# Two chained cross-attentions: VectorE's product of the semantic result moved ahead of the maxima, the sums copied right behind it, fewer unread products in the tail

## The chip, the cores and the metric

The kernel runs on one core of one Trainium2 chip. Its time is the device time of the core in microseconds (us); the number compared is the median of several runs. A profile is one execution taken by the hardware profiler: it has a start and an end for each instruction of TensorE (PE, with its weight loads PEld), VectorE (DVE), ScalarE (ACT) and GpSimd (POOL), and for the DMAs that SyncE (SP) issues.

## The reference

Two attention layers follow each other. Each has 64 batches of 256 tokens with 320 channels, and 20 heads of 16. All is float32. Layer 0 attends to 77 text tokens. (Its image part has no tokens: the context has 77 rows, all of them text.) Layer 1 takes the last 4 of the 77 as image tokens and the other 73 as text:

```python
# layer 0
q, k, v = heads(x @ Wq.T), heads(ctx @ Wk.T), heads(ctx @ Wv.T)
x = x + merge(softmax(q k^T / 4) v) @ Wo.T + bo
# layer 1
text, ip = ctx[:, :-4], ctx[:, -4:]
probs_t  = softmax(q k_t^T / 4)                 # 73 text tokens
text_out = probs_t v_t
qsem     = l2norm(probs_t @ text)               # per head, 512 wide
sem      = qsem @ l2norm(ip)^T                  # 4 numbers per head and token
probs_ip = softmax(q k_ip^T / 4 + 0.5 * sem) * spatial_mask
x = x + (text_out + probs_ip v_ip) @ W_out + b_out
```

## The kernel before, in words

The 64 batches go in 32 pairs p. A pair is cut into 10 units for each layer: a unit is 8 heads (or, for the last heads, 4 heads of both halves) of 128 tokens of one batch. The main loop runs over steps g; k = g % 10 is the place in the period. In step g layer 0 works on unit g and layer 1 on unit g - 13 (`LAG` is 13). The code calls layer 0 and layer 1 `l` = 0 and 1.

The semantic part of layer 1 doesn't compute `qsem` in 512 channels. A Gram matrix of the context (`gram`, `place_gram`: line L512 and the copies L516, L517) stands in tile `gv` beside the values and a column of ones. The matmuls of `semantics` (L774, L781) multiply the transposed exponentials of the step before with it and give, per head, 73 columns (exponentials times Gram matrix, the *semantic result*) and 21 more columns (products with the image rows, the values and the sum). `weighted` multiplies the 73 columns on VectorE with the exponentials (`prod`, L792 and L795), a later reduction (`nrm`, L1130) makes the squared norm of it, and `sums_out` copies the other 21 columns on ScalarE (`sums`, L1057).

One PSUM tile, `sc`, of 4 banks, takes all of a step: the semantic result of the unit that is one step further, and the scores of both layers (L659). There is a single buffer of it, so the matmuls of the next step wait until all readers of this step have done. The readers of `sc` are, for each layer, the maxima (`mx`, L677) and the difference from them (`w`, L679), both on VectorE and both in `shifted`; the product; and the copy of the sums.

The order of each engine's instructions is that of the program: `keep_order` ties each instruction to the one before it on its engine. Within a step it is this, in the kernel before:

- TensorE: `sc` (semantics, scores of layer 0, scores of layer 1); the transposes of layer 1's exponentials (`tr`, `rtr`: L723, L724); the first fillers; the transposes of layer 0's normalized exponentials; the second fillers, and for some units the value products `pv` (L809, L814, in `attend`).
- VectorE: `mx`, `w` of layer 0; `mx`, `w` of layer 1; at k = 1 and 6 the maxima `most` (L890) of the image scores; the product; the sums `sm` of layer 0's exponentials (L705), their reciprocal (L706); `nrm`; then, at some k, the small work of the image part, and the additions of the projections to `x` (L617, four in a row, and L636).
- ScalarE: copies left from the step before (queries L602, outputs L945 and L946); `pt` and `pr` of layer 1 (the copies of its transposes out of PSUM, L730 and L731); the exponential of layer 0 (L687); copies of the first fillers (`kT` L348, `q` L589, `vs` L391, `gram` L516 and L517); `pt` and `pr` of layer 0 (L749 and L750, or L738 and L741); the copy of the sums; the exponentials of layer 1 (`parts`, L690 and L691); copies of the second fillers and of `pv`; every fifth step a square root (L875) and back to the exponential (L877), each with a load of its function table. At k = 5 the exponential of layer 0 stands behind the layer-0 copies. At k = 1 and 6 the copy of the sums stands ahead of the layer-0 copies.
- GpSimd: placing of keys and values, `att` (L694, reads layer 1's `w`), and the products `parts` of layer 0 (L710), which wait for `sm`.

*Fillers* are the projections that lie around the attention: keys, queries, values, outputs, Gram matrices. `fillers(k, p)` lists them by k in three groups. Their PSUM tiles come from two pools with two buffers each: `pms` (projections `k_ps`, `q_ps`, `v_ps`, `o_ps`, `g_ps`, and most `pv`) and `ptr` (all transposes, `itr` L915 and `ltr` L928 among them). A matmul that takes a buffer waits for the copy that empties it: for example layer 0's transposes take the buffers of layer 1's, and wait for the copies `pt` and `pr` of these.

In the tail, when layer 0 has no unit left (from step 323 on), `keep_busy` issues transposes of the identity that nobody reads (`busy`, L759): 14 in each of 10 steps in which layer 1 still has a unit, and other numbers behind these.

Of the kernel before, what the change touches and what calls it, by code (L numbers as in the profile page):

```python
# [70 lines left out]
def tile_two_cross_attentions(ctx: ExitStack, tc: tile.TileContext, a: dict, out: bass.AP):  # L71
# [143 lines left out]
    def load_more(g):  # L215
        queue = nc.sync
        if g == 1:
            queue.dma_start(cip, cip_in.rearrange("(k p) t -> p k t", p=P))
            load_ctx_weight("wkip1", queue, wkip)
        elif g == 3:  # L220
            load_ctx_weight("wvip1", queue, wvip)
        elif g == 5:
            wo[0], bo[0] = load_out("wo0", queue), load_bias("bo0", queue)
        elif g == 6:
            wq[1] = load_chan("wq1", queue)
        elif g == 8:
            wo[1], bo[1] = load_out("wo1", queue), load_bias("bo1", queue)
            queue.dma_start(smask, a["smask"])
# [416 lines left out]
    def eight(t, u):  # L645

        return t[:, PLACES[u] : PLACES[u] + 8].rearrange("p (r e) ... -> p r e ...", e=2)
# [16 lines left out]
    def shifted(ps, l, p, b, u):  # L664


        nt = (T, TT)[l]
        name = f"{l}_{p}_{b}{u}"
        if l and u == 0:
            stats[p, b] = (  # L670
                small.tile([P, 2 * H, NIP], F32, tag="att", name=f"att{p}_{b}", bufs=3),
                big.tile([P, 2 * H, NIP + D + 1], F32, tag="sums", name=f"sums{p}_{b}", bufs=3),
                small.tile([P, 2 * H], F32, tag="nrm", name=f"nrm{p}_{b}", bufs=3),
            )
        sc = ps[:, :, 2 * T * l : 2 * T * (l + 1)].rearrange("p r (e t) -> p r e t", t=T)
        mx = small.tile([P, 4, 2], F32, tag="mx", name=f"mx{name}")
        nc.vector.tensor_reduce(mx, sc[:, :, :, :nt], AX.X, ALU.max)  # L677
        w = ws[l] = sp.tile([P, 4, 2, T], F32, tag=f"w{l}", name=f"w{name}", bufs=2 - l)
        nc.vector.tensor_tensor(  # L679
            w, sc, mx.unsqueeze(3).broadcast_to([P, 4, 2, T]), ALU.subtract  # L680
        )

    def exponential(l, g, p, b, u):

        w = ws[l]
        if not l:
            nc.scalar.activation(w, w, AF.Exp, scale=SCALE)  # L687
            return
        two = ws[l] = parts1[g % 3]
        nc.scalar.activation(two[:, :4].rearrange("p (e a) j t -> p (a j) e t", e=2), w[:, :, :, :M], AF.Exp, scale=SCALE)  # L690
        nc.scalar.activation(  # L691
            rests(two), w[:, :, :, M:TT], AF.Exp, scale=SCALE
        )
        nc.gpsimd.tensor_copy(eight(stats[p, b][0], u), w[:, :, :, TT:])  # L694

    def rests(two):

        r = two[:, 4].rearrange("p j (a c) -> p (j a) c", c=QR)
        return r[:, :, : 2 * R1].rearrange("p r (e t) -> p r e t", e=2)
# [52 lines left out]
    def keep_busy(n, pool=ptr, tag="tr"):  # L752


        if n:
            ps = pool.tile([P, 4, P], F32, tag=tag, name=f"busy{len(busy)}")
            busy.append(n)
            for i in range(n):
                nc.tensor.transpose(ps[:, i % 4, :], ident, ident)  # L759
# [26 lines left out]
    def by_block(ps):  # L786
        return ps[:, :, SEM0 : SEM0 + 2 * GV].rearrange("p r (e t) -> p r e t", t=GV)

    def weighted(ps, p, b, u, w):
        sm = by_block(ps)  # L790
        prod = sp.tile([P, 4, 2, TT], F32, tag="prod", name=f"prod{p}_{b}{u}", bufs=1)
        nc.vector.tensor_tensor(  # L792
            prod[:, :, :, :M], sm[:, :, :, :M], w[:, :4].rearrange("p (e a) j t -> p (a j) e t", e=2), ALU.mult
        )
        nc.vector.tensor_tensor(prod[:, :, :, M:], sm[:, :, :, M:TT], rests(w), ALU.mult)  # L795
        return prod
# [70 lines left out]
    def image_squares(p, b):  # L867
        total, r = stats[p, b][1][:, :, NIP + D], stats[p, b][2]
        t = small.tile([P, 2 * H], F32, tag="least", name=f"least{p}_{b}", bufs=1)
        nc.vector.tensor_mul(t, total, total)  # L870
        nc.vector.scalar_tensor_tensor(r, t, EPS * EPS, r, ALU.mult, ALU.max)

    def image_norm(p, b):
        r = stats[p, b][2]
        nc.scalar.activation(r, r, AF.Sqrt, scale=(SCALE / SEM) ** 2)  # L875

        nc.scalar.activation(one, r[:, :1], AF.Exp, scale=0.0)  # L877
# [167 lines left out]
    def unit(g):  # L1045
        return (g // NU, g % NU // BU, g % BU) if 0 <= g < NP * NU else None
# [9 lines left out]
    def sums_out(ps):  # L1056
        nc.scalar.copy(eight(stats[before1[:2]][1], before1[2]), by_block(ps)[:, :, :, TT:])  # L1057
# [3 lines left out]
    for g in range(NP * NU + LAG + 12):  # L1061
        p, k = divmod(g, NU)
        first, second, third = fillers(k, p)
        if g == NU + 3:
            in_order = len(nc.cur_bb.bb.instructions)
        load_more(g)
        now = [unit(g), unit(g - LAG)]
        ps = prod = None
        for fn, args in early.pop(g, ()):
            fn(*args)  # L1070
        drains = [fn for what in ("i", "q", "o") if what in held for fn in held.pop(what)()]
        for fn in drains:
            fn()
        if now[0] or now[1] or before1:
            ps = psc.tile([P, 4, 512], F32, tag="sc", name=f"sc{g}")
            todo = []
            if before1:
                todo.append((semantics, (*before1[:3], before1[4])))
            for l in range(2):
                if now[l]:  # L1080
                    todo.append((scores, (l, *now[l])))
            for n, (fn, args) in enumerate(todo):
                fn(ps, n == 0, n == len(todo) - 1, *args)
        ends = before1 and before1[2] == BU - 1
        for l in range(2):
            if now[l]:
                shifted(ps, l, *now[l])
        if g in middle:
            fn, args = middle.pop(g)
            fn(*args)  # L1090
        new1 = None
        if last1:
            transposed(1, *last1)
            new1 = (*last1, pts[1])
        if now[0] and k != 5:
            exponential(0, g, *now[0])
        if k == 2:
            for fn, args in first:
                fn(*args)
        if before1:  # L1100
            prod = weighted(ps, *before1[:4])
        if k != 2:
            for fn, args in first:
                fn(*args)
        if before1 and k in (1, 6):
            sums_out(ps)
        if last0:
            transposed(0, *last0)
        idle = g - NP * NU
        if idle > 2:  # L1110
            keep_busy(14 if now[1] else {13: 12, 14: 16, 15: 14, 16: 16, 17: 16}.get(idle, 0))
        if idle == 17:
            fn, args = second.pop(0)
            fn(*args)
            keep_busy(8)
        if now[0] and k == 5:
            exponential(0, g, *now[0])
        if before1 and k not in (1, 6):
            sums_out(ps)
        for fn, args in between.pop(g, ()):  # L1120
            fn(*args)
        if now[1]:
            exponential(1, g, *now[1])
        if now[0]:
            normalize(g)
        for fn, args in later.pop(g, ()):
            fn(*args)
        if before1:
            q, b, u = before1[:3]
            nc.vector.tensor_reduce(eight(stats[q, b][2], u), prod, AX.X, ALU.add)  # L1130
            if ends:
                image_squares(q, b)
                text_output(q, b)
                later[g + 1] = [(image_scores, (q, b))]
                middle[g + 2] = (image_shifted, (q, b))
                between[g + 2] = [(image_exponential, (q, b))]
                (early if b else later)[g + 3] = [(image_weights, (q, b))]
        for fn, args in second:
            fn(*args)
        if last0:  # L1140
            q, b, u, _ = last0
            if u == 1 or u == BU - 1:
                attend(q, b, int(u > 1))
        for fn, args in third:
            fn(*args)
        if g in (6, 7, 9, 10, 18, 19) or -6 <= idle <= -2:
            keep_busy(8, pms, "ms")
        if ends:
            image_norm(*before1[:2])
        last0 = (*now[0], ws[0]) if now[0] else None  # L1150
        before1 = new1
        last1 = (*now[1], ws[1]) if now[1] else None
# [51 lines left out]
```

## Time and profile before

| | us |
|---|---|
| median of 3 runs | 2474.95 (2473.02 to 2475.86) |
| the profiled execution's own time | 2474.45 |
| its span, first to last instruction | 2472.7 |
| PE busy | 2394.2 (97%) |
| DVE busy | 1987.4 (80%) |
| ACT busy | 1482.2 (60%) |
| POOL busy | 1370.9 (55%) |
| `prod` L792 and L795, mean of one | 0.681 and 0.223 |
| `mx` L677 and `w` L679, mean of one | 0.776 and 0.800 |
| `sums` L1057, mean of one | 0.301 |
| `w` L687 (exponential of layer 0), mean of one | 0.719 |
| `busy` L759, in all | 39.9 (310 transposes) |

How to read the profile. A line of the waits says who waited, for whom, then the total in us, how often, and the longest. A line of the timeline has the start in us, the duration, the engine, the line of the kernel, the operation, the tiles written and read with their shapes, and in brackets the idle time of the engine ahead of it and what ended it. Matmuls are pipelined and their ends are modelled; neighbours on one engine overlap by some hundredths of a us. The granted clock of TensorE was 0.999 of full speed.

### The profile page before, as it was taken

How to read it: one execution, taken by the hardware profiler on the slowest of the kernel's cores; microseconds unless marked ns; L12 is line 12 of the kernel's file. 1: busy time of each engine (PE TensorE's matmuls, PEld its weight loads, DVE VectorE, ACT ScalarE, POOL GpSimd, SP SyncE). 2: the span in 40 equal slices, each digit the busy share in tenths (PEclk: the TensorE clock that was granted, in tenths of full speed). 3: DMA queues.
4: the chain of work that ended last, by engine and by line, in shares of the span. 5: the costliest groups of instructions: out<-in, count | busy, mean ns of one | idle time of the engine just before them, and what ended most of it. 6: DMA issues, size and time to landing. Idle time of an engine off the chain costs nothing.

```text
span 2472.7 us, 100470 instructions
## 1 busy us (share of the span) xinstructions
PE 2394.2 (97%) x41118; PEld 1847.9 (75%) x41118; DVE 1987.4 (80%) x3673; ACT 1482.2 (60%) x3767; POOL 1370.9 (55%) x3483
## 2 busy tenths in 40 slices
PE   7899999999999999999999999999999999999888
PEld 5677777777777777777777777777777777777676
DVE  3588788888888888888888888888888888888864
ACT  3466666666666666666665666665665666666543
POOL 2455565566555656555656555556555556555542
PEclk9999999999999999999999999999999999999999
DMA  6212111112111112111121211121211121211000
GB/s 173 75 30 57 50 52 47 56 53 58 52 57 41 54 54 59 52 52 51 47 59 56 62 45 48 46 60 56 62 44 48 47 59 56 61 39 39 26 23 25
DMA packets 150914, 131.83 MB, mean 53 GB/s; under 512 B 45432, under 2 KB 129144, under 8 KB 150456
## 3 DMA queue, kind: packets, MB, share of 16 engines
q1 hardware_dynamic: 149592, 124.27, 17.5%
q8 instruction: 325, 5.32, 0.9%
q10 hardware_dynamic: 864, 1.15, 0.2%
q14 instruction: 133, 1.09, 0.1%
HBM read 87.43 MB, written 33.91 MB: 49 GB/s over the span
## 4 chain that ended last, share of the span: by engine, by line
PE 76%; DVE 12%; ACT 3%; DMA 3%; POOL 2%; issue 1%; SPq 1%; DVEq 0%; POOLq 0%; ACTq 0%
PE tr L723 10%; PE sc L774 9%; PE o_ps L547 8%; PE q_ps L547 8%; PE sc L659 7%; DVE w L679 5%; PE v_ps L390 4%; PE sc L781 4%; PE o_ps L632 3%; DVE mx L677 3%; PE k_ps L345 3%; PE pv L809 2%; PE q_ps L557 2%; PE o_ps L557 2%; PE q_ps L575 2%; PE pv L814 2%
## 5 line engine op out<-in xcount | busy, mean ns | idle before, releaser
L677 DVE TENSOR_REDUCE mx<-sc 128x8 f32<-128x584 f32 (+1 forms) x640 | 496.6, 776 | 342.1 <-PE sc L659 339.3
L710 POOL TENSOR_TENSOR parts<-w,sm 128x512 f32<-128x512 f32 (+1 forms) x640 | 440.6, 709 | 437.1 <-DVE sm L706 144.2
L679 DVE TENSOR_TENSOR w<-sc,mx 128x616 f32<-128x616 f32 x640 | 511.8, 800 | 73.0 <-DVE mx L677 1.4
L723 PE MATMUL tr<-ident,parts 128*128 128x128 f32 x2560 | 407.5, 282 | 9.5 <-ACT pt L730 5.6
L730 ACT COPY pt<-tr 128x512 f32<-128x512 f32 x320 | 187.1, 585 | 323.8 <-PE tr L723 318.9
L723 PEld LDWEIGHTS tr<-ident,parts 128*128 128x128 f32 x2560 | 284.2, 140 | 128.6 <-issue 83.1
L687 ACT ACTIVATE w<-w 128x616 f32<-128x616 f32 x320 | 230.1, 719 | 143.7 <-DVE w L679 142.7
L774 PEld LDWEIGHTS sc<-gv,pt 64*64 64x64 f32 x10240 | 233.5, 133 | 105.6 <-ACT sums L1057 52.7
L774 PE MATMUL sc<-gv,pt 64*64 64x94 f32 x10240 | 277.9, 245 | 23.6 <-ACT sums L1057 23.0
L694 POOL COPY att<-w 128x32 f32<-128x32 f32 x320 | 67.0, 209 | 354.6 <-DVE w L679 350.8
L705 DVE TENSOR_REDUCE sm<-w 128x8 f32<-128x616 f32 x320 | 250.9, 784 | 13.9 <-ACT w L687 13.8
L659 PE MATMUL sc<-kbd,q 32*64 32x154 f32 x10240 | 247.7, 293 | 1.1 <-ACT q L602 1.0
L547 PE MATMUL q_ps<-x,wq 128*128 128x256 f32 x1024 | 232.9, 380 | 5.3 <-ACT kT L348 5.3
L547 PE MATMUL o_ps<-aT,wo 128*128 128x256 f32 x1024 | 231.8, 379 | 0.7 <-ACT aT L945 0.7
L1057 ACT COPY sums<-sc 128x168 f32<-128x168 f32 x320 | 96.2, 301 | 225.8 <-DVE prod L795 223.9
L1130 DVE TENSOR_REDUCE nrm<-prod 128x8 f32<-128x584 f32 x320 | 226.7, 709 | 0.3
L792 DVE TENSOR_TENSOR prod<-sc,parts 128x512 f32<-128x512 f32 x320 | 217.9, 681 | 2.8 <-PE sc L781 2.8
L547 PEld LDWEIGHTS q_ps<-x,wq 128*128 128x128 f32 x1024 | 189.2, 190 | 30.2 <-ACT kT L348 7.3
L547 PEld LDWEIGHTS o_ps<-aT,wo 128*128 128x128 f32 x1024 | 189.6, 190 | 24.4 <-ACT aT L945 1.1
L690 ACT ACTIVATE parts<-w 128x512 f32<-128x512 f32 x320 | 206.4, 645 | 0.0
L749 ACT COPY pt<-tr 128x512 f32<-128x512 f32 x256 | 150.3, 587 | 66.9 <-PE tr L723 65.5
L390 PE MATMUL v_ps<-wv,cf 128*128 128x320 f32 (+1 forms) x624 | 179.2, 433 | 0.0
(144 smaller groups left out, 4560.3 us busy)
## 6 DMA issues: line engine op xcount, KB each, us to landing
out_dram<-x SPq DMA_DIRECT2D x64, 256.0 KB
x<-in_x_dram SPq DMA_DIRECT2D x31, 512.0 KB
v_rows<-vs SPq DMA_DIRECT2D x38, 320.0 KB
vm<-v_rows SPq DMA_DIRECT2D x152, 80.0 KB
ct<-in_ctx_dram SPq DMA_DIRECT2D x32, 308.0 KB
cf<-in_ctx_dram SPq DMA_DIRECT2D x38, 256.0 KB
g_rest<-gram_rest SPq DMA_DIRECT2D x512, 0.5 KB
v_rest<-v_rows SPq DMA_DIRECT2D x448, 11.2 KB
```

The source lines that it names most:

```text
L390: nc.tensor.matmul(ps[:n, :C], cfs[i][:, k, :n], wv[l][:, k, :], start=(k == 0), stop=(k == KE - 1))
L547: nc.tensor.matmul(ps[b][:, m, :], w[:, k, m * P : (m + 1) * P], main[:, k, b * S : (b + 1) * S], start=(k == 0 and m == 0), stop=False,)
L659: nc.tensor.matmul(ps[c, r, 2 * T * l : 2 * T * (l + 1)], tokens[rows, c], kbd[rows, part].rearrange("p e t -> p (e t)"), start=start, sto ...
L677: nc.vector.tensor_reduce(mx, sc[:, :, :, :nt], AX.X, ALU.max)
L679: nc.vector.tensor_tensor(w, sc, mx.unsqueeze(3).broadcast_to([P, 4, 2, T]), ALU.subtract)
L687: nc.scalar.activation(w, w, AF.Exp, scale=SCALE)
L705: nc.vector.tensor_reduce(sm, w, AX.X, ALU.add)
L710: nc.gpsimd.tensor_tensor(two[:, 8 * t0 : 8 * t1].rearrange("p (h t) -> p h t", h=8), w[:, :, t0:t1], sm.unsqueeze(2).broadcast_to([P, 8, ...
L723: nc.tensor.transpose(ps[:, i, :], flat[:, i * P : (i + 1) * P], ident)
L774: nc.tensor.matmul(ps[c, i % 2 * 2 + j, at : at + GV], pt[half_rows, i, c], gv[b][half_rows, part, i, :], start=start and i < 2, stop=False,)
L792: nc.vector.tensor_tensor(prod[:, :, :, :M], sm[:, :, :, :M], w[:, :4].rearrange("p (e a) j t -> p (a j) e t", e=2), ALU.mult)
L1130: nc.vector.tensor_reduce(eight(stats[q, b][2], u), prod, AX.X, ALU.add)
```

## The change

`weighted` and `sums_out` are called right behind the matmuls of `sc`, ahead of `shifted`, in every step. On VectorE the two instructions of the product come first in the step, then the maxima and differences of the layers. On ScalarE the copy of the sums stands behind the copies left from the step before and ahead of `pt` of layer 1, where it stood behind the copies of layer 0 (at k = 1 and 6: ahead of these). The special cases of k = 2 and of k = 1 and 6 go. In the tail `keep_busy` issues 8 transposes in each of the ten steps instead of 14. The numbers of all instructions but these transposes are the same.

```diff
         ends = before1 and before1[2] == BU - 1
+        if before1:
+            prod = weighted(ps, *before1[:4])
+            sums_out(ps)
         for l in range(2):
             if now[l]:
                 shifted(ps, l, *now[l])
...
         if now[0] and k != 5:
             exponential(0, g, *now[0])
-        if k == 2:
-            for fn, args in first:
-                fn(*args)
-        if before1:
-            prod = weighted(ps, *before1[:4])
-        if k != 2:
-            for fn, args in first:
-                fn(*args)
-        if before1 and k in (1, 6):
-            sums_out(ps)
+        for fn, args in first:
+            fn(*args)
         if last0:
             transposed(0, *last0)
         idle = g - NP * NU
         if idle > 2:
-            keep_busy(14 if now[1] else {13: 12, 14: 16, 15: 14, 16: 16, 17: 16}.get(idle, 0))
+            keep_busy(8 if now[1] else {13: 12, 14: 16, 15: 14, 16: 16, 17: 16}.get(idle, 0))
...
         if now[0] and k == 5:
             exponential(0, g, *now[0])
-        if before1 and k not in (1, 6):
-            sums_out(ps)
```

## The prediction

> **What bounds it now.** I read the page first, then the waits, then the timeline of whole steps. A step is one round of the main loop; ten (k = 0 to 9) make a period of 72.8 us (windows view, 1181.15 to 1253.97). R is the end of a step's last `sc` matmul; the times of steps below count from R.
>
> ```profile
> PE 2394.2 (97%) x41118; PEld 1847.9 (75%) x41118; DVE 1987.4 (80%) x3673; ACT 1482.2 (60%) x3767; POOL 1370.9 (55%) x3483
> ...
> PE 76%; DVE 12%; ACT 3%; DMA 3%; POOL 2%; issue 1%; SPq 1%; DVEq 0%; POOLq 0%; ACTq 0%
> ```
>
> TensorE is the bound, with VectorE second on the chain. So the question is who TensorE nearly waits for. The waits:
>
> ```profile
> DVE mx L677 <- PE sc L659: 339.3, 221, 14.5
> ...
> ACT sums L1057 <- DVE prod L795: 223.9, 243, 3.4
> ...
> PEld sc L774 <- ACT sums L1057: 52.7, 99, 1.6
> ...
> PEld pv L809 <- ACT pr L750: 11.5, 30, 0.4
> ...
> PEld pv L809 <- ACT gram_rest L517: 6.1, 29, 0.6
> ```
>
> The reader is to see two things. VectorE has 339.3 us of room ahead of its maxima, about 1 us a step. And TensorE is already on the edge of three ScalarE copies, with tiny waits once a period: any delay of those copies is paid in full. Now a step of k = 7 (R = 1232.50) and, last two lines, one of k = 0 (R = 1253.97):
>
> ```profile
> 1232.01 0.49 PE L659 MATMUL sc<-kbd,q 32*64 32x154 f32 x15
> ...
> 1232.58 0.80 DVE L677 TENSOR_REDUCE mx<-sc 128x8 f32<-128x616 f32 x1
> ...
> 1234.31 0.72 ACT L687 ACTIVATE w<-w 128x616 f32<-128x616 f32 x1 [0.37 <-DVE w L679]
> ...
> 1235.10 0.59 ACT L749 COPY pt<-tr 128x512 f32<-128x512 f32 x1
> ...
> 1235.74 0.88 PE L915 MATMUL itr<-ident,iw 128*80 128x128 f32 x4
> ...
> 1236.33 0.22 DVE L795 TENSOR_TENSOR prod<-sc,parts 128x72 f32<-128x72 f32 x1
> ...
> 1236.59 0.30 ACT L1057 COPY sums<-sc 128x168 f32<-128x168 f32 x1 [0.74 <-DVE prod L795]
> ...
> 1257.37 0.16 ACT L517 COPY gram_rest<-g_ps 73x13 f32<-73x13 f32 x1
> ...
> 1257.59 0.64 PE L809 MATMUL pv<-pt,v 128*32 128x256 f32 x8
> ```
>
> ScalarE works in order: the exponential L687 waits for `w` of layer 0, and behind it stand copies that free PSUM for TensorE. `itr` starts 0.05 after `pt` ends; `pv` starts 0.06 after `gram_rest`.
>
> **The change, part by part.** A plain step now: `mx` at 0.08, `w` of layer 0 ends 1.78, L687 runs 1.88-2.59, `w` of layer 1 ends 3.39, `prod` ends 4.13, `sums` 4.16-4.46, next `sc` from 4.51. The product (L792 and L795) costs 0.82 (0.08 less overlapped), whether first or last. What differs is the wait. In the built program the layer-0 maxima wait for the `sums` copy, the next `sc` for the layer-1 `w`, and the product still for the last `sc` matmul. So after: `prod` 0.08-0.90, `sums` 0.93-1.23 (the 0.03 and 0.30 of the row above), `mx` at 1.27 (0.04 on, much like the 0.05 from `sums` to the next `sc`), `w` 0 ends 2.97, L687 3.07-3.79, `w` 1 ends 4.58, next `sc` from 4.63. VectorE stands idle 0.37 a step for the copy, its later sums L705 come 0.46 later, and L687 with all behind it 1.2 later. `pt` of layer 1, now behind `sums`, ends at 1.73 instead of 1.26.
>
> That both reads take turns is how the trace has it: 243 times `sums` waited for `prod`, though `sc` had been complete for 4 us. Bounds of the handover: 0 if the readers could overlap, 0.37 as derived, 0.5 with a further 0.1; I take 0.37, from the nearest row. The Trainium skill (PSUM — Partial Sum Buffer, "PSUM bank collisions raise a hardware error") says that ScalarE and VectorE must not touch one bank and quadrant together, reads included; it speaks against this change, and without it the sum would be that of the third rival below.
>
> Step by step, with TensorE's own row first:
> k = 1 and 3: nothing. In k = 1 `o_ps` L547 keeps TensorE until 3.99; in k = 3 half of `q_ps` L547 runs until 4.43, and the copy it needs (L589) ends 4.05.
> k = 4: the layer-0 transposes began at 1.53; they need `pt`, 1.73 + 0.05: +0.25.
> k = 5: ScalarE comes from the square root's two table loads (1.28 each) and two `q` copies; these end 0.47 later, less the 0.25 by which step 4 is longer: 1.43 instead of 1.20. `sums` ends 1.66, `w` 1 ends 5.01, next `sc` 5.06 instead of 4.51: +0.55.
> k = 6: next `sc` was at 4.74, because `most` (L890) stood ahead of the product; now 4.63: -0.11. VectorE ends 0.46 later, 0.68 into step 7.
> k = 7: `prod` ends 1.50, `sums` 1.83, `w` 0 3.50, L687 4.32, `kT` 4.49, `pt` 4.97, `itr` 5.02 instead of 3.24: +1.78. In 6 of 30 periods step 6 is 8.2 long (two more `v_ps`), VectorE is in time, and it is +1.18.
> k = 8: `vs` L391 ends 4.11 (was 3.31), then `pt` 4.64; `ltr` L928 begins 4.68 instead of 4.11: +0.55; half that in the 6.
> k = 9: the next `sc` waited for `sums` (ends 5.58, behind `pt`); in k = 1, with the same matmuls, it starts 0.18 earlier: -0.18.
> k = 0: VectorE's four L617 of step 9 end at 1.70 instead of 1.06 (0.46 later, the step 0.18 shorter). From there `prod` 2.52, `sums` 2.85, `w` 0 4.59, L687 5.41, `gram_rest` 5.57, `pv` 5.62 instead of 3.63: +2.0. The largest term.
> k = 2: VectorE is 0.70 late (0.17-0.26 before; `most` and the L617 of step 1); L687 ends 4.27, `pt` 4.75, `pv` 4.80 instead of 3.79: +1.0.
>
> A full period: 2.0 + 0 + 1.0 + 0 + 0.25 + 0.55 - 0.11 + 1.78 + 0.55 - 0.18 = 5.84, or 8%. Semantic results exist from step 15, layer-0 exponentials until step 319. Count: k = 0, 29 x 2.0 = 58; k = 2, 30; k = 4, 30 x 0.25 = 7.5; k = 5, 31 x 0.55 = 17; k = 6, -2.6; k = 7, 24 x 1.78 + 6 x 1.18 + 1 = 50.8; k = 8, 14.9; k = 9, -5.4. Together +170.
>
> The rest at nothing, with its cover. GpSimd's `parts` L710 end at most 0.5-1.1 later, but the layer-0 transposes need them only 1.5 into the next step. SP issues the same DMAs in the same order; those of `gram` leave 2 us later in k = 0 and are needed by `gv` L530 eight steps on. At k = 2 `first` holds only L632 and L636, which VectorE gets after both maxima as before. The tail: 10 steps lose 6 transposes of 0.125 (1.75 for 14), 7.5 us of TensorE. But they start behind `pt`, now 0.47 later, and the next `sc` waits for `w` 1 at about 2410.85 where it had `sums` at 2410.72: nothing, within -7.5 and +3. With less fill TensorE pauses longer there; its longest wait on `pt` is now 2.2 us and the windows view still shows a granted clock of 1.00 from 2380 to 2400.
>
> The Trainium skill (TensorE: Matmul & The Clock Gate, "What's actually happening") lets the clock halve after an idle window of about 3.4 us. My pauses are 2 us at most, so by the page too nothing is added; if each period did lose one window it would be, as an estimate from that page, some 1.7 us x 30 = 51 us more.
>
> The profiled execution took 2474.45 (span 2472.7), 0.5 below the median of 2474.95. 2474.45 + 170 = 2644.5, against the median 2645.
>
> **Rivals.** First, that only VectorE's ring counts, and the copies behind L687 have more room than the edges show (a wait of 0.05 could be chance). Then only steps where VectorE is late pay: k = 0 +0.44 (`w` 1 then sets the next `sc`), k = 5 +0.13, k = 7 +0.08, k = 6 -0.11: about 0.55 x 30 = +17, 2492. Against it: the 29 and 30 waits of `pv`, once a period, and `itr`.
>
> Second, faster: the release of `sc` decides. If the maxima followed the product directly and L687's delay of 0.82 were covered, `w` 1 would end 4.13 and the next `sc` start at 4.18: k = 5 -0.33, k = 6 -0.35 (TensorE's own 4.39), k = 9 -0.18, 0.86 x 30 = 26, with 7.5 of the tail 2441. It decides once exp L687 may come 0.82 later without a wait at k = 0, 2 and 7, where the rows show 0.06, 0.44 and 0.05 of room.
>
> Third, the readers are not kept apart, but ScalarE's queue is as I read it: L687 0.8 later, k = 0 about +1.1, k = 7 +1.1, k = 2 +0.4, less the gains: about 2.1 x 30 = +65, 2540. The same time would come if the product ran beside the `sc` matmuls, the change then doing more than the built waits let it.
>
> Fourth, all handovers cost 0.1 more and the lateness piles up: seven paying steps x 0.2 x 30 = +42, 2690, or above 2705 if the layer-1 `kT` copy (0.07 of room in k = 4) also misses.
>
> **How the numbers follow.** Mine 0.77, the first rival 0.06, faster 0.04, the third 0.06, the fourth 0.06, no change 0.01. The range 2575 to 2705 takes in my sum with 40% off its terms below and the fourth rival's 2690 above. A measurement of this kernel tells about 0.2% (5 us) from no change; so faster 0.04, same 0.01, slower 0.95.
>
> **What would show it.** Right: `ACT sums <- DVE prod` falls from 223.9 us to some tens; `DVE mx <- ACT sums` appears with about 300 waits of 0.37; `DVE mx <- PE sc` goes, and `prod <- PE sc` takes its place; L687 waits longer for `w`; TensorE shows waits of 1-2 us on `gram_rest` (k = 0), `pt` at `itr` (k = 7) and at `pv` (k = 2); TensorE's share falls to about 90% at an unchanged granted clock; the period is near 78.6. Wrong: `mx` starting without the copy, `pv` and `itr` starting where they did, or a period below 75.

## The result, and the profile after

The changed kernel takes 2638.62 us (median of 4 runs, 2637.01 to 2641.29), the kernel before in the same runs 2474.39. The ratio is 1.0665, 95% interval 1.0646 to 1.0683: slower, by 164 us, where the forecast said 2645. The page, busy time and the chain that ended last:

```profile
PE 2407.9 (91%) x41058; PEld 1843.1 (70%) x41058; DVE 2011.7 (76%) x3673; ACT 1478.4 (56%) x3767; POOL 1373.5 (52%) x3483
...
DVE 45%; PE 34%; ACT 10%; issue 4%; DMA 3%; POOL 2%; SPq 1%; DVEq 0%; ACTq 0%; POOLq 0%
```

No engine does noticeably more work. TensorE's share fell from 97% to 91%, and the chain, 76% TensorE before, now runs mainly through VectorE. The waits:

```profile
ACT sums L1057 <- DVE prod L795: 486.2, 292, 4.8
ACT w L687 <- DVE w L679: 341.2, 287, 3.7
DVE prod L792 <- PE sc L659: 316.6, 201, 5.1
...
DVE mx L677 <- ACT sums L1057: 139.8, 318, 1.7
...
PE tr L723 <- ACT pt L730: 43.8, 100, 2.7
PEld pv L809 <- ACT gram_rest L517: 42.1, 29, 1.5
...
PEld pv L809 <- ACT pt L749: 33.7, 32, 1.1
PEld itr L915 <- ACT pt L749: 31.0, 30, 1.9
```

The room that VectorE had ahead of its maxima (339.3 us) now stands ahead of the product (316.6). New is the turn-taking: the maxima wait 318 times for the sums, 0.44 each. And three ScalarE copies for which TensorE's weight loads had hardly waited (6.1, 0.6 and 4.9 us in all, in the order of the lines) now hold them up by 1.0 to 1.5 us each, once a period. TensorE's transposes of layer 0 wait 100 times for `pt` of layer 1 (L730), where they waited 6 times before (5.6 us). One step of k = 7 (the last `sc` matmul ends at 1312.16), from the timeline:

```profile
1313.28 0.22 DVE L795 TENSOR_TENSOR prod<-sc,parts 128x72 f32<-128x72 f32 x1
...
1313.59 0.30 ACT L1057 COPY sums<-sc 128x168 f32<-128x168 f32 x1 [1.22 <-DVE prod L795]
...
1313.92 0.80 DVE L677 TENSOR_REDUCE mx<-sc 128x8 f32<-128x616 f32 x1 [0.42 <-ACT sums L1057]
...
1315.65 0.72 ACT L687 ACTIVATE w<-w 128x616 f32<-128x616 f32 x1 [1.10 <-DVE w L679]
...
1316.44 0.59 ACT L749 COPY pt<-tr 128x512 f32<-128x512 f32 x1
...
1317.08 0.64 PE L915 MATMUL itr<-ident,iw 128*80 128x128 f32 x4 [0.77 <-ACT pt L749]
```

This is the forecast's path link by link: product, sums, maxima, exponential, `pt`, and TensorE at the end of it. `itr` starts at 4.92 where it started at 3.24, and 5.02 was forecast. At k = 0 (that end is 1257.00) it is `gram_rest` and `pv`:

```profile
1262.34 0.16 ACT L517 COPY gram_rest<-g_ps 73x13 f32<-73x13 f32 x1
...
1262.55 0.64 PE L809 MATMUL pv<-pt,v 128*32 128x256 f32 x8 [1.20 <-ACT gram_rest L517]
```

`pv` starts at 5.55 instead of 3.63; 5.62 was forecast.

Below, a step's length is the time from the end of its last `sc` matmul to the end of the next step's, in the profiled execution, the median over the steps of one k. The steps 15 to 319 took 2248.1 before and 2412.0 after (+163.9); what lies ahead of them changed by -1.0, what lies behind by +1.6. So the loss is in the main loop.

### The profile page after: what moved, and what is told of

It is laid out like the page before. It is cut to its first block, busy times and chain, and to the rows that moved or that the text cites. A ratio compares the mean times of both kernels' runs of the same rounds, so it can differ in the third digit from the quotient of the medians.

```text
span 2637.3 us, 100892 instructions
## 1 busy us (share of the span) xinstructions
PE 2407.9 (91%) x41058; PEld 1843.1 (70%) x41058; DVE 2011.7 (76%) x3673; ACT 1478.4 (56%) x3767; POOL 1373.5 (52%) x3483
## 4 chain that ended last, share of the span: by engine, by line
DVE 45%; PE 34%; ACT 10%; issue 4%; DMA 3%; POOL 2%; SPq 1%; DVEq 0%; ACTq 0%; POOLq 0%
DVE w L679 12%; DVE mx L677 11%; DVE prod L792 6%; PE sc L774 5%; PE q_ps L547 4%; PE sc L659 4%; DVE sm L705 4%; DVE nrm L1123 3%; DVE x L617 3%; ACT sums L1057 3%; PE pv L809 3%; ACT w L687 2%; PE v_ps L390 2%; PE pv L814 2%; PE tr L723 2%
## 5 line engine op out<-in xcount | busy, mean ns | idle before, releaser
L677 DVE TENSOR_REDUCE mx<-sc 128x8 f32<-128x584 f32 (+1 forms) x640 | 497.7, 778 | 178.7 <-ACT sums L1057 139.8
L792 DVE TENSOR_TENSOR prod<-sc,parts 128x512 f32<-128x512 f32 x320 | 218.7, 684 | 322.7 <-PE sc L659 316.6
L723 PE MATMUL tr<-ident,parts 128*128 128x128 f32 x2560 | 409.9, 283 | 48.1 <-ACT pt L730 43.8
L687 ACT ACTIVATE w<-w 128x616 f32<-128x616 f32 x320 | 229.8, 718 | 341.2 <-DVE w L679 341.2
L723 PEld LDWEIGHTS tr<-ident,parts 128*128 128x128 f32 x2560 | 278.8, 141 | 185.8 <-issue 116.5
L1057 ACT COPY sums<-sc 128x168 f32<-128x168 f32 x320 | 96.0, 300 | 486.9 <-DVE prod L795 486.2
L730 ACT COPY pt<-tr 128x512 f32<-128x512 f32 x320 | 189.7, 593 | 0.7 <-PE tr L723 0.7
```

The lines of the kernel that those rows point to most:

```text
L723: nc.tensor.transpose(ps[:, i, :], flat[:, i * P : (i + 1) * P], ident)
L792: nc.vector.tensor_tensor(prod[:, :, :, :M], sm[:, :, :, :M], w[:, :4].rearrange("p (e a) j t -> p (a j) e t", e=2), ALU.mult)
```

## The experiments

### One half of the edit at a time

**The product alone.** `weighted` ahead of `shifted`, the sums where they were, 8 transposes in the tail:

```diff
+        if before1:
+            prod = weighted(ps, *before1[:4])
         for l in range(2):
             if now[l]:
                 shifted(ps, l, *now[l])
```

> The product stands ahead of the maxima in every step; the copy of the sums stays where it was, behind the layer-0 copies (k = 1 and 6: ahead of them), and so waits for the layer-1 w. The maxima follow the product without a wait. Theory 1 (ScalarE's ordered queue: the exponential L687 comes later, and TensorE pays for the copies behind it): L687 starts 0.78 later than in the kernel before, pv at k = 0 starts +0.85, itr at k = 7 +0.77, pv at k = 2 +0.2, and k = 6 gains 0.23: about +51, 2526 us. Theory 2 (VectorE's ring of maxima and product is the bound after the change, and what it lost is the wait for the copy in each step): without the wait VectorE has what it had, so 2468 to 2476 us.

Measured: 2511.16, ratio 1.0154 (1.0139 to 1.0169). **The sums alone**, with the product in its old place and 14 transposes:

```diff
+        if before1:
+            sums_out(ps)
         for l in range(2):
             if now[l]:
                 shifted(ps, l, *now[l])
```

> The kernel before, with the copy of the sums alone ahead of the maxima in every step; the product stays behind them. The maxima wait for a ScalarE copy that needs only the last matmul of sc. Theory 1: mx of layer 0 starts at 0.47 in plain steps (0.08 before), but where ScalarE comes late from the square root it waits longer, 2.25 at k = 0 and 1.55 at k = 5; steps k = 0 +1.27, 5 +1.14, 7 +0.38, 8 +0.25, 9 -0.18: +86, 2560 us. Theory 2 (the wait for the copy, each step, is what the change costs VectorE): the wait is there in full, so about the time after the change, 2620 to 2645 us.

Measured: 2546.97, ratio 1.0297 (1.028 to 1.0314). Changes of the step lengths, in us:

| k | forecast | both (the change) | product alone | sums alone |
|---|---|---|---|---|
| 0 | +2.0 | +1.92 | +0.69 | +1.17 |
| 2 | +1.0 | +1.16 | +0.15 | 0 |
| 4 | +0.25 | +0.43 | 0 | 0 |
| 5 | +0.55 | +0.31 | -0.01 | +1.29 |
| 6 | -0.11 | -0.01 | -0.22 | -0.03 |
| 7 | +1.78 | +1.44 | +0.59 | +0.34 |
| 8 | +0.55 | +0.64 | +0.13 | -0.01 |
| 9 | -0.18 | -0.23 | 0 | -0.24 |
| sum | 5.84 | 5.66 | 1.33 | 2.52 |

k = 1 and 3 are unchanged in all of them. In the main loop the product alone cost 43.6, the sums alone 76.6, both together 163.9, which is 43.7 more than the two. What the two share is room: that ahead of the copies, and VectorE's own. At k = 2 `pv` started 0.44 after `pt`: the product alone makes L687 0.80 later there and pays 0.15, the sums alone make it 0.36 later and pay nothing, and with both it is 1.81 later, more than the sum of the two, since VectorE also comes late into the step (its first reader of `sc` starts at 0.73, before at 0.17); 1.16 is paid. At k = 4 neither alone costs anything: only when the copy of the sums stands ahead of `pt` of layer 1 and itself waits for the product does `pt` come late enough for TensorE. With the product alone the same waits show, that of `pv` smaller:

```profile
PEld itr L915 <- ACT pt L749: 29.1, 30, 2.0
PEld pv L809 <- ACT gram_rest L517: 27.1, 29, 0.9
```

The sums alone hold up the maxima where ScalarE is late: at k = 0 behind a table load (`mx` starts at 2.13, though VectorE's L617 end at 1.58) and at k = 5 behind the two `q` copies (1.73 instead of 0.08). At k = 5 the product is last and ends at 5.74, and the next `sc` waits for it; the waits of `mx` in that run:

```profile
DVE mx L677 <- ACT sums L1057: 390.6, 262, 5.6
```

My expectation was 2526 and 2560; both came out about 14 lower, the other theories' 2468 to 2476 and 2620 to 2645 are far off.

### Where k = 0 loses 1.92

**The change at k = 0 alone:**

```diff
+        ahead = before1 and k == 0
+        if ahead:
+            prod = weighted(ps, *before1[:4])
+            sums_out(ps)
```

> The kernel before, with product and sums ahead of the maxima at k = 0 alone (one step in ten). Theory 1: no lateness is handed over from step 9, so pv at k = 0 starts 1.29 later instead of the 1.92 of the whole change, all other steps stay: 29 x 1.29 = 37, 2511 us. Theory 2: VectorE's ring at k = 0 ends with the layer-1 w at 5.55 where TensorE is ready at 5.51, so +0.1 a period, 2477 us.

Measured: 2511.29, ratio 1.0154 (1.0139 to 1.0169), as theory 1 had it; k = 0 is 8.48 long (+1.24), all others as before. **The changed kernel with k = 9 in its old order:**

```diff
-        if before1:
+        ahead = before1 and k != 9
+        if ahead:
             prod = weighted(ps, *before1[:4])
             sums_out(ps)
...
+        if before1 and not ahead:
+            prod = weighted(ps, *before1[:4])
...
+        if before1 and not ahead:
+            sums_out(ps)
```

> The changed kernel, but step k = 9 keeps the order of before (product behind the maxima, sums behind layer 0's copies). Theory 1 (part of what k = 0 loses is lateness of VectorE and ScalarE that step 9 hands over): k = 9 loses its gain, 7.23 to 7.46 us, and k = 0 falls from 9.16 to about 8.5, as in the version with the change at k = 0 alone (8.48); together 30 x (0.23 - 0.66) = -13 us, the time about 2626. Theory 2 (k = 0's loss is all its own): k = 0 stays at 9.16, k = 9 loses 0.23, 30 x 0.23 = 7 us, the time about 2645.

Measured: 2630.07, ratio 1.0625 (1.0609 to 1.0641). k = 9 goes from 7.23 to 7.46 and k = 0 from 9.16 to 8.45: so 0.7 of k = 0's loss is made in step 9. There VectorE ends later and TensorE earlier, and the L617 end at 1.01 instead of 1.73 into step 0. The main loop fell by 10.5; 13 was expected.

### How much is ScalarE's queue

**The exponential L687 behind the copies** that free PSUM (first fillers and `pt` of layer 0), at the six k where they are due:

```diff
-        if now[0] and k != 5:
+        if now[0] and k not in (0, 2, 4, 5, 7, 8):
             exponential(0, g, *now[0])
...
-        if now[0] and k == 5:
+        if now[0] and k in (0, 2, 4, 5, 7, 8):
             exponential(0, g, *now[0])
```

> The kernel after the change, but the exponential L687 of layer 0 stands behind the copies of the first fillers and of the layer-0 transposes at k = 0, 2, 4, 5, 7 and 8 (after the change it stands so at k = 5 alone). VectorE's order and its wait for the copy of the sums are untouched. Theory 1: TensorE's waits on gram_rest, on pt at itr and on pt at pv go, what stays is pt of layer 1 behind the sums and VectorE's lateness; steps against before k = 0 +0.75, 2 +0.5, 4 +0.4, 5 +0.3, 7 +0.75, 8 0, 9 -0.2: +75, 2550 us. Theory 2: VectorE does the same as after the change, 2630 to 2640 us.

Measured: 2577.98, ratio 1.0423 (1.0408 to 1.0439). That gives back 60.6 of the 164; theory 1 had expected 2550, and most of what is missing lies at k = 2. k = 0 falls from 9.16 to 8.21, k = 7 from 8.23 to 7.35, k = 8 from 7.87 to 7.23. TensorE's waits for these copies at `pv` and `itr` shrink to under 1 us in the whole run. But behind them the next limit stands. At k = 7, and at k = 2 too, layer 0's transposes wait for `pt` of layer 1, which stands behind the sums (at k = 7 they begin at 2.36 instead of 1.59, at k = 2 at 2.94 instead of 2.07). At k = 0 it is VectorE: `w` of layer 1 ends at 6.41, and the next `sc` starts at 6.47. At k = 2, which did not fall at all (8.33), the last wait is for L636, queued behind both maxima:

```profile
1248.24 0.48 DVE L636 SCALAR_TENSOR_TENSOR x<-o_ps,bo,x 128x256 f32<-128x256 f32 x1
...
1248.77 0.66 PE L584 MATMUL q_ps<-x,wq 128*64 128x128 f32 x8 [0.30 <-DVE x L636]
```

**L636 moved ahead of layer 1's maxima, first try.** `project_last` is called between the two layers at k = 2:

```diff
         for l in range(2):
+            if l and k == 2:
+                for fn, args in first:
+                    fn(*args)
             if now[l]:
                 shifted(ps, l, *now[l])
```

> The version with the exponential behind the PSUM-freeing copies (2577.98 us), and at k = 2 also project_last's fillers moved between layer 0's and layer 1's maxima, so that VectorE's L636 runs ahead of layer 1's mx and w. Theory 1 (in that version k = 2 lost 1.22 us because q_ps L584 waited for VectorE's late L636): k = 2 falls from 8.33 to about 7.95 us, 30 x 0.38 = 11 us, the time about 2567. Theory 2 (TensorE's own chain at k = 2, or the next sc's wait for w, sets it): k = 2 stays at 8.3 and the time at 2576 to 2580.

Measured: 2594.05, ratio 1.0481 (1.0463 to 1.0498), a miss of both. The edit moved more than L636: its 12 matmuls went ahead of layer 1's transposes on TensorE, which now started at 2.39 instead of 0.10, and every copy behind them came 0.9 later. k = 2 took 8.88. `q_ps` no longer waited for L636, so the run could not decide between the two theories. **Second try**, with layer 1's transposes issued first, so that TensorE's order is unchanged:

```diff
             if l and k == 2:
+                if last1:
+                    transposed(1, *last1)
+                    new1 = (*last1, pts[1])
                 for fn, args in first:
                     fn(*args)
```

> The version with the exponential behind the copies (2577.98 us), and at k = 2 the transposes of layer 1 and then project_last's fillers issued between layer 0's and layer 1's maxima: TensorE's order is that of 2577.98, only VectorE's L636 comes ahead of layer 1's mx and w. Theory 1 (in that version q_ps L584's wait for L636 is what k = 2 still loses, and in the run before this one the late layer-1 transposes hid it): L636 ends near 4.4, q_ps starts behind pv at 5.63, the next sc at 6.22; k = 2 falls from 8.33 to 7.96 us, 30 x 0.37 = 11 us, the time about 2567. Theory 2 (VectorE's lateness is in the step whatever the order): w of layer 1 or another wait holds the next sc at 6.6, k = 2 stays at 8.3, 2576 to 2580.

Measured: 2572.59 (2570.98 to 2577.68), ratio 1.0396 (1.0382 to 1.041); this interval and that of 2577.98 touch, so the gain is read from the step. k = 2 is 7.98 long, as theory 1 had it, and `q_ps` starts behind `pv`, which itself is late because `pt` of layer 1 is:

```profile
1246.53 0.59 ACT L730 COPY pt<-tr 128x512 f32<-128x512 f32 x1
...
1247.26 0.63 PE L723 MATMUL tr<-ident,parts 128*128 128x128 f32 x4 [0.49 <-ACT pt L730]
...
1248.21 0.48 DVE L636 SCALAR_TENSOR_TENSOR x<-o_ps,bo,x 128x256 f32<-128x256 f32 x1
...
1249.95 0.66 PE L584 MATMUL q_ps<-x,wq 128*64 128x128 f32 x8
```

So of the 1.22 that k = 2 still lost, L636 was worth 0.35; the other 0.87 stands, by these rows, with the late `pt` of layer 1. Of 30 x 0.35 = 10.5 only 5.4 reached the median. The profiled execution, the slowest of the four (2577.68), shows one way in which it is lost: four steps of k = 4 grew by 0.8 to 1.0 each (9.91 to 10.90 in one) and a fifth by 0.4. In such a step the waits lead back to a transfer:

```profile
1649.51 0.72 POOL L464 TENSOR_TENSOR v<-vm,half 128x320 f32<-128x320 f32 x1 [5.27 <-DMA vm<-v_rows]
...
1651.12 0.70 POOL L376 TENSOR_TENSOR kbd<-kT,head_mask 128x308 f32<-128x308 f32 x1
...
1651.86 0.28 ACT L348 COPY kT<-k_ps 128x146 f32<-128x146 f32 x1 [4.09 <-POOL kbd L376]
...
1652.20 1.99 PE L547 MATMUL q_ps<-x,wq 128*128 128x256 f32 x8 [1.99 <-ACT kT L348]
```

GpSimd waits for `vm`, the key copy for GpSimd, and the query matmuls for the buffer that this copy frees. That a step which starts sooner waits longer for the same transfer is a reading that was not tested, and how much the other three runs lost in this way was not profiled.

### The tail

**The kernel before with 8 transposes** instead of 14 in the ten tail steps (no other edit), and **the changed kernel with 14**:

```diff
-            keep_busy(14 if now[1] else
+            keep_busy(8 if now[1] else
```

> The kernel before with 8 unread transposes instead of 14 in the ten steps of the tail, nothing else. Theory 1: they stand behind pt of layer 1 and the next sc waits for the sums anyway, so 2471 to 2475 us (0 to -2). Theory 2: TensorE sets the end in the tail, so all 7.5 us of the transposes are gained: 2466 us. If TensorE's clock falls for want of fill, the time rises above 2476 and the granted clock of the windows from 2380 on is under 1.00.

```diff
-            keep_busy(8 if now[1] else
+            keep_busy(14 if now[1] else
```

> The changed kernel with 14 transposes in each tail step as before. The forecast said the shorter tail is worth nothing, within -7.5 and +3: 2637 to 2640. The rival reading: it saves 3.7 us as it did in the kernel before, so that with 14 the time is about 2642.

Measured: 2471.91, ratio 0.9985 (0.9976 to 0.9994); and 2647.59, ratio 1.0696 (1.0682 to 1.0711). The shorter tail is worth about 4 us in the kernel before, between the 0 to 2 and the 7.5 of my theories, and 9 in the changed one (8 by the ratios; 5.4 in the parts of the two profiles behind step 319). For the changed kernel both theories (2637 to 2640, and 2642) missed 2647.59. In the changed kernel the transposes begin behind the later `pt`, and 14 of them end after `w` is ready. The same step with 14, and then with 8:

```profile
2561.79 1.75 PE L759 MATMUL busy<-ident 128*128 128x128 f32 x14 [1.17 <-ACT pt L730]
...
2563.47 0.88 PE L774 MATMUL sc<-gv,pt 64*64 64x94 f32 x32
```

```profile
2558.24 1.09 PE L759 MATMUL busy<-ident 128*128 128x128 f32 x8 [1.17 <-ACT pt L730]
...
2559.46 0.88 PE L774 MATMUL sc<-gv,pt 64*64 64x94 f32 x32
```

Counted from the last `sc` matmul, `sc` starts at 3.54 with 14 and at 3.08 with 8, when `w` of layer 1 is ready.

### Is a faster version to be had

What gained in the table is k = 9 (sums early) and k = 6 (maxima `most`, L890, behind the product). **Only these two, in the kernel before**, and **the two with the shorter tail**:

```diff
-        if g in middle:
-            fn, args = middle.pop(g)
-            fn(*args)
...
+        if g in middle:
+            fn, args = middle.pop(g)
+            fn(*args)
...
-        if before1 and k in (1, 6):
+        if before1 and k in (1, 6, 9):
             sums_out(ps)
```

> The kernel before with two of its own waits taken away: at k = 9 the copy of the sums stands ahead of the layer-0 copies (as at k = 1 and 6), and at k = 1 and 6 the maxima most (L890) stand behind the product. No wait of the maxima on ScalarE. Theory 1 (the change's small gains at k = 9 and 6 are the earlier release of sc, its losses all from what L687 and VectorE get late): k = 9 -0.23 x 30, k = 6 -0.22 x 24: -12, 2461 us. Theory 2 (the gain at k = 9 came with the longer period, as slack from other steps): no change, 2471 to 2475 us.

```diff
-            keep_busy(14 if now[1] else
+            keep_busy(8 if now[1] else
```

> The run before this one with the tail's 8 transposes as well. Both theories: the sum of the two runs' differences, 2459 to 2461 us by theory 1; if the tail gains 7.5, 2453 us.

Measured: 2476.2, ratio 1.0004 (0.9995 to 1.0012), no change; and 2472.13, ratio 0.9986 (0.9977 to 0.9994), the tail's gain alone. Both gains that were expected (to 2461, and to 2459 to 2461) were missed; theory 2 came near the time of the first, but not by its reason, since k = 9 and 6 did fall, by 0.23 and 0.22, and k = 0 and 7 grew by 0.26 and 0.24. Step 0 of that run (the last `sc` matmul of step 9 ends at 1255.18):

```profile
1254.94 1.55 DVE L617 SCALAR_TENSOR_TENSOR x<-o_ps,bo,x 128x256 f32<-128x256 f32 x4
...
1256.42 0.78 DVE L677 TENSOR_REDUCE mx<-sc 128x8 f32<-128x616 f32 x1
...
1258.14 0.72 ACT L687 ACTIVATE w<-w 128x616 f32<-128x616 f32 x1 [0.40 <-DVE w L679]
...
1258.86 0.16 ACT L517 COPY gram_rest<-g_ps 73x13 f32<-73x13 f32 x1
...
1259.07 0.64 PE L809 MATMUL pv<-pt,v 128*32 128x256 f32 x8
```

`sc` is ready 0.23 earlier, but VectorE is not: its L617 end 1.31 into the step instead of 1.06, and the chain to `gram_rest` and `pv` is as late in absolute time as before. The best version of all is the kernel before with the shorter tail, 2471.91: it beats both kernels, the one before by only 0.15%.

## Why the prediction was right, point by point

**The wait.** `mx` waits for `sums` in every step: 0.37 forecast, 0.42 in a plain step and 0.44 on average (139.8 / 318). The copy starts 0.09 behind the product, where the row of before had 0.03; why was not settled. `w` of layer 1 ends at 4.61 in a plain step (4.58 forecast).

**The steps.** 0 and 8 are within 0.1. 7 was put 0.34 too high, in two parts: VectorE entered the step 0.10 less late, which is the 0.10 of `itr`; and `itr` itself takes 0.64 when it starts late, where its row of before has 0.88, and I had moved the 0.88 with it. 4 and 5 were mis-sized against each other: at k = 4 the transposes started 0.15 behind `pt`, not 0.05, and `pt` ended at 1.78, not 1.73 (+0.43 for +0.25); the longer step 4 let ScalarE's `q` copies end at 1.26 of step 5, not 1.43 (+0.31 for +0.55). Together 0.74 for 0.80. 2 was 0.16 too low: `pv` started at 4.94, not 4.80. At k = 6 the gain of 0.11 did not come (-0.01): VectorE entered that step 0.06 late, the turn took 0.42, and `w` of layer 1 ended at 4.67, not 4.58. The medians make 5.66 a period for 5.84, and the main loop lost 163.9 for 170. That the sum came out so close is partly luck. Over all steps k = 5 and 7 lost 9.7 and 44.5 us for 17 and 50.8, and k = 2, 4 and 6 lost 34.5, 10.1 and 0.2 for 30, 7.5 and a gain of 2.6; these misses nearly cancel.

**What I held to cost nothing.** For L636 at k = 2 the cover held in the changed kernel itself, since `pt` was as late; it was worth 0.35 a period as soon as that cover was gone (2577.98 against 2572.59). The tail's reckoning held in size, +1.6 for "nothing, within -7.5 and +3", but it is the sum of two terms that I did not price: the new order costs the tail about 7.0 (115.0 behind step 319 with 14 transposes, against 108.0), and the fewer transposes return 5.4.

**What I said the profile would show, and it didn't.** `ACT sums <- DVE prod` was to fall to some tens; it rose from 223.9 to 486.2, since ScalarE, with nothing else queued ahead of the copy, stands there for the whole product. This idling is not free: `pt` of layer 1 stands behind the copy, and TensorE's waits for it rose from 5.6 to 43.8 us. The sum had this as the term of k = 4; the sign did not follow from it. The other signs came: `prod <- PE sc` in the place of `mx <- PE sc`, TensorE's weight loads waiting 1.0 to 1.5 us at k = 0, 2 and 7, 91% for "about 90%", a period of 78.5 for 78.6, and the granted clock at 0.997. The clock was not lowered once a period: the windows view shows 1.00 from 1257 to 1335.

**The rivals.** The first (2492, only VectorE counts) falls with the waits on `gram_rest` and `pt`, and with the 60.6 us that reordering ScalarE's queue gave back. It holds a share of truth: with that queue mended 104 us remain, 29 of them (30 x 0.97) at k = 0, where VectorE's `w` is then the last wait, and 37 (30 x 1.22) at k = 2, of which VectorE's L636 holds 0.35 a period and the late `pt` of layer 1 the rest. The second (2441) falls with the product alone: there the maxima did follow the product directly, and it took 2511. The third (2540) needed the readers to overlap; the maxima waited for the copy in 318 of the 320 steps. The fourth needed 0.1 more in every handover; 0.07 was found in all, and no lateness beyond what the forecast had.

## What to carry to other kernels

When a read of a shared PSUM tile is moved ahead, what counts is who stands behind the displaced instruction on every in-order queue: here 0.82 of product and 0.44 of turn-taking put one exponential 1.2 later, and TensorE waits for the copies queued behind it; putting these ahead of it gave back 61 of the 164 us. Slack is used once, on the copies and on VectorE itself: two edits that each fit partly into the room cost more together (164) than apart (44 and 77), and a step that is let go earlier gives it back in the next if the engine that is late there is no earlier. Before moving a call to test a wait, compare the order on every engine: the first try on L636 moved twelve matmuls too.

## What the runs showed of the hardware that was not expected

TensorE ran at half speed behind a pause of 2.00 us in one profiled execution, and at full speed behind the same pause in two others. The rows of `busy` are, for the kernel before, for the same kernel with 8 transposes in the tail, and for the run that also has the sums early at k = 9 and `most` behind the product:

```profile
2399.58 1.75 PE L759 MATMUL busy<-ident 128*128 128x128 f32 x14 [2.00 <-ACT pt L730]
```

```profile
2401.43 1.97 PE L759 MATMUL busy<-ident 128*128 128x128 f32 x8 [2.00 <-ACT pt L730]
```

```profile
2402.61 1.09 PE L759 MATMUL busy<-ident 128*128 128x128 f32 x8 [2.00 <-ACT pt L730]
```

That is 0.125, 0.246 and 0.136 us for one transpose. The windows view shows it as a granted clock of 0.91 where the kernel before had 1.00 (and the third run 1.00). The two lines, before first (then us, busy time and count of PE, PEld, DVE, ACT and POOL, clock, DMA share, GB/s):

```profile
2400.00:2420.00 20.00, 18.04 (x366) 14.97 (x364) 10.98 (x20) 8.33 (x24) 9.42 (x33) 1.00 0.03 8
```

```profile
2400.00:2420.00 20.00, 15.88 (x305) 13.00 (x305) 12.26 (x23) 9.29 (x28) 8.48 (x30) 0.91 0.02 4
```

Such windows are not peculiar to the shorter tail. The kernel before has 0.91 from 2340 to 2360 and from 2440 to 2460, and the changed kernel has one at 0.91 in its tail with 8 transposes and with 14. In the profiled execution with 8 transposes the tail step of these rows takes 7.14 instead of 6.35 with less work in it; five of the ten tail steps gain 0.50 to 0.66 there, and four 0.06 or nothing. That execution (2474.72) was the slowest of the eleven, so how much the lower clock takes from the median gain of 4 us is not shown.

The Trainium skill (TensorE: Matmul & The Clock Gate, "What's actually happening") has the clock halve after an idle window of about 3.4 us. The pause here is shorter than that window, so by these rows the lower clock does not need a wholly idle one. Neither the pause nor the number of transposes decides by itself: the same pause, with 8 transposes behind it, left the clock alone in the third run. What does decide was not tested.
